# Two attention blocks: folded weight products moved ahead of everything, loads in chunks, biases as rows

## The chip, the cores and the metric

The kernel runs on one core of a Trainium2 chip. The metric is device time in microseconds (us), as the median of runs of the whole program. All data are 32-bit floats. The engines are TensorE (PE in the profile, with its weight loads shown apart as PEld), VectorE (DVE), ScalarE (ACT), GpSimd (POOL) and SyncE (SP), which here only issues transfers. Matmuls write to PSUM, of which this kernel uses banks under two tags, "s" and "o", with two buffers each; a buffer holds two banks of 128x512.

## The reference

Two blocks run one after the other on x of shape (8, 512, 32, 32): eight images, 512 channels, 1024 positions.

```python
# block 0: group norm of 32 groups, 8 heads of 64
h = group_norm(x, norm_w, norm_b)
qkv = einsum('oc,bchw->bohw', qkv_w, h) + qkv_b
attn = softmax(einsum('bhnd,bhmd->bhnm', q, k) / sqrt(64))
o = einsum('bhnm,bhmd->bhnd', attn, v)
x = x + einsum('oc,bchw->bohw', proj_w, o) + proj_b
# block 1: norm over the whole sample, one head of 512
n = norm(x) * gn_gamma + gn_beta
q, k, v = wq @ n + bq, wk @ n + bk, wv @ n + bv
attn = softmax(einsum('bci,bcj->bij', q, k) * 512**-0.5)
out = einsum('bcj,bij->bci', v, attn)
x = x + wo @ out + bo
```

## The kernel before

**Folded weights.** Block 1 has one head, so its query and key weights are multiplied into one matrix, "wqk1", and its value and output weights into another, "wvo1". `product` (L513) makes each of them on the chip by 16 matmuls of 128x512, which the trace shows as 32 passes, since a matmul of 32-bit floats is two. The biases that result are also made on the chip. `bias_through` (L485) multiplies a 512x512 matrix by a bias vector: 16 matmuls of a 128x128 stationary tile with a moving operand of one column (32 passes). It is used for "bias1" (wo1 with the value bias), "bias_q1" (nk1 with the query bias) and "bias0" (block 0's projection with its value bias).

**Strassen-like multiplication.** All large weight multiplications go through `strassen` (L369), with seven products instead of eight. A weight is held as a `Weight` tile of seven parts. A11, A12 and A22 are loaded, A21 goes to a tile called "rest", and `finish` (L171) makes S1 to S4 from them with four DVE operations. `Weight.finish` (L205) also writes the tile to DRAM ("stored"), and later images load it from there. There are three buffers for weight tiles. On the side of the data, `Combined` makes T1 to T4 from the quarters of x. `strassen` takes a bank tagged "s" (the line) and one tagged "o" (the single), copies the line out on ACT and adds on DVE.

**Order.** PE, ACT and DVE follow the order of the program text (a manual schedule). `at_steps` runs the steps of one or two interleaved multiplications and calls hooks between them, so work of other stages is put between the steps by hand. Before the first image:

1. SP loads nv1 and wo1, ACT's queue loads x of image 0; then the weights qk02 (ACT) and v0 (SP), then nq1 (ACT) and nk1 (SP). At most eight transfers are in flight: each issue waits for the one eight places earlier.
2. DVE takes the statistics of x (`of_half`, L291).
3. PE makes wvo1 and bias1, then the mean and variance products (L262); DVE and GpSimd turn them into scale and shift, and ACT and DVE normalise x (`normed`, L330, L332).
4. DVE finishes qk02 and v0 and makes T1 to T4; PE runs the first q and k stage (`pairs_qk`, heads' pairs 0 and 2).

Image 0 then runs `layer0`. First comes the value stage (`make_v`), between whose steps DVE takes the statistics of the next image's x. Only for image 0, `product` then makes wqk1 and bias_q1, the weights qk13 and p0 are finished, and bias0 is made. The second q and k stage (pairs 1 and 3) follows, then the attention: scores (L606), exponentials (L533), sums (L535), values (L625) and key sums (L639). The latter multiply by a tile of ones with 32 columns, which land in four different strips of 32 partitions. The projection (ps_p, L432) and block 1 come last. Images 1 to 7 repeat this with stored weights.

SP's transfers keep their own order; each waits for what it stores, for the buffer it fills, and for the transfer eight places earlier.

Of the kernel before, what the change touches and what calls it, by code (L numbers as in the profile page):

```python
# [40 lines left out]
P = 128  # L41
# [18 lines left out]
def two_attention_blocks(  # L60
# [3 lines left out]
    x: bass.AP,  # L64
    w_qkv0: bass.AP,
    w_proj0: bass.AP,
    n_q1: bass.AP,
# [22 lines left out]
    def banks(tag, name):  # L90
        return psum.tile([P, 2, HALF], FP, tag=tag, name=name)

    def tile2(name):
        return tpool.tile([P, 2, HALF], FP, tag="t", name=name)
# [18 lines left out]
    def load_x(b, queue):  # L113
        xs = quarters_of(f"x_{b}")
        for half in range(2):
            for i in range(2):
                queue.dma_start(xs[i][half], quarter_of(x, b, i, half))
        return xs

    def load_raw(src, name, queue):  # L120

        chunks = []
        for half in range(2):
            t = tile2(f"{name}_{half}")
            rows = src[half * 2 * P : (half + 1) * 2 * P]
            queue.dma_start(t, rows.rearrange("(cc p) o -> p cc o", p=P))
            chunks += [t[:, 0, :], t[:, 1, :]]
        return chunks

    vec = const.tile([P, 12 * NC], FP, tag="vec", name="vec")  # L130
    nc.scalar.dma_start(vec, vectors)
    nv1, wo1 = load_raw(n_v1, "nv1", nc.sync), load_raw(w_o1, "wo1", nc.sync)
    xs_next = load_x(0, nc.scalar)

# [45 lines left out]
    class Weight:  # L180

        def __init__(self, name, sources):
            self.name, self.sources = name, sources
            self.tile = wpool.tile([P, W_SIZE], FP, tag="w", name=f"w_{name}")
            self.parts, self.rest, at = [], [], 0
            for src, col, width in sources:
                size = len(A_PARTS) * 2 * width
                self.parts.append(parts_of(self.tile[:, at : at + size], width))  # L190
                at += size
            if name in stored:
                nc.sync.dma_start(self.tile, stored[name])

        def load(self, queue):
            for (src, col, width), parts in zip(self.sources, self.parts):
                rest = tile2(f"rest_{self.name}")[:, :, :width]
                self.rest.append(rest)
                for i in range(2):
                    for j in range(2):  # L200
                        cols = src[j * 2 * P : (j + 1) * 2 * P, i * 2 * P + col : i * 2 * P + col + width]
                        to = rest if (i, j) == (1, 0) else parts[f"A{i + 1}{j + 1}"]
                        queue.dma_start(to, cols.rearrange("(k p) o -> p k o", p=P))

# [5 lines left out]

    WQ0, WK0, WV0 = (w_qkv0[:, i * C : (i + 1) * C] for i in range(3))
    SOURCES = {
        "qk02": [(WQ0, 0, P), (WK0, 0, P)],
        "qk13": [(WQ0, P, P), (WK0, P, P)],
        "v0": [(WV0, 0, 2 * P)],
        "p0": [(w_proj0, 0, 2 * P)],
        "wqk1": [(None, 0, 2 * P)],
        "wvo1": [(None, 0, 2 * P)],
    }

    def load_first(name, queue):
        w = Weight(name, SOURCES[name])
        w.load(queue)
        return w

    waiting = [load_first("qk02", nc.scalar), load_first("v0", nc.sync)]
    nq1, nk1 = load_raw(n_q1, "nq1", nc.scalar), load_raw(n_k1, "nk1", nc.sync)


# [6 lines left out]
    def next_weight():  # L236

        w = waiting.pop(0)
        if coming:
            name = coming.pop(0)  # L240
            waiting.append(Weight(name, SOURCES[name]) if name in stored else load_first(name, nc.sync))
        return w
# [241 lines left out]

    def bias_through(w, v_bias, bias, name):  # L485


        t = const.tile([P, NC], FP, tag=name, name=name)
        ps = banks("s", f"ps_{name}")[:, 0, :]
        for oc in range(NC):  # L490
            for cc in range(NC):
                nc.tensor.matmul(  # L492
                    ps[:, oc : oc + 1], w(cc, oc), vec[:, v_bias + cc : v_bias + cc + 1],
                    start=cc == 0, stop=cc == NC - 1,
                )
        if bias is None:
            nc.vector.tensor_copy(t, ps[:, :NC])
        else:
            nc.vector.tensor_tensor(t, ps[:, :NC], vec[:, bias : bias + NC], ALU.add)
        return t  # L500

    def square_of(chunks):
        return lambda cc, oc: chunks[cc][:, oc * P : (oc + 1) * P]

    def square_of_parts(w):
        def square(cc, oc):
            i, j = oc // 2, cc // 2
            a = w.rest[0] if (i, j) == (1, 0) else w.parts[0][f"A{i + 1}{j + 1}"]
            return a[:, cc % 2, oc % 2 * P : (oc % 2 + 1) * P]

        return square

    def product(a, b, name):  # L513

        w = Weight(name, SOURCES[name])
        w.rest = [tile2(f"rest_{name}")[:, :, : 2 * P]]
        for j in range(2):
            ps = banks("o", f"ps_{name}_{j}")
            for k in range(2):
                to = 2 * j + k  # L520
                for cc in range(NC):
                    nc.tensor.matmul(  # L522
                        ps[:, k, :], a[cc][:, to * P : (to + 1) * P], b[cc],
                        start=cc == 0, stop=cc == NC - 1,
                    )
            evacuate(w.parts[0][f"A1{j + 1}"], ps[:, :, : 2 * P])
            evacuate(w.parts[0]["A22"] if j else w.rest[0], ps[:, :, 2 * P :])
        w.finish()

# [48 lines left out]
    def layer0(bs, qs, ks, b, load_next, norm_next):  # L578
# [12 lines left out]
        if b == 0:  # L591
            product(nq1, nk1, "wqk1")
            made["bias_q1"] = bias_through(square_of(nk1), V_BQ1, None, "bias_q1")

# [59 lines left out]
        if b == 0:  # L654
            w.finish()
            waiting[0].finish()
            made["bias0"] = bias_through(square_of_parts(waiting[0]), V_BV0, V_BP0, "bias0")
        hooks = {8: [lambda: score(0)], 9: [lambda: score(1)]}
# [25 lines left out]
        for i in range(2, len(units) + 2):  # L684
# [25 lines left out]
            if pair in spreads and (g, kt) == (1, NT - 1):  # L710
                for g in range(2):
                    divide(pair, g, spreads[pair][:, g, :])

        bias = made["bias0"]

# [193 lines left out]

    made = {}  # L910


    with tc.manual_schedule(engines={PE, ACT, DVE}):
        norm = norm0(xs_next, 0)
        for cc in range(NC):
            norm.of_half(cc, 0)
            norm.of_half(cc, 1)
            norm.of_channels(cc)
        product(nv1, wo1, "wvo1")
        made["bias1"] = bias_through(square_of(wo1), V_BV1, V_BO1, "bias1")  # L920
        norm.mean_of_all()
        norm.variance_of_all()
        norm.normed(xs_next)
        for w in waiting:
            w.finish()
        bs = combined(xs_next, "0_0")
        qs, ks = [None] * NC, [None] * NC
        at_steps(together(*pairs_qk(next_weight(), 0, bs, qs, ks, 0)), {})
        for b in range(B):
# [443 lines left out]
```

## Time and profile before

| | |
|---|---|
| runs | 2965.56, 2965.85, 2968.4 us; median 2965.85 |
| profiled execution: time | 2973.16 us |
| profiled execution: span | 2971.3 us |
| mean granted clock of TensorE | 0.993 |
| first matmul of the program | 10.33 us after the span's start |
| first value stage of image 0 | from 67.23 us |
| wqk1's product | from 91.40 us |
| second q and k stage of image 0 | from 116.31 us |

Durations are read from the profiled execution, and places in it are us from its span's start. A wait is idle time of an engine just before an instruction, with the engine and line, or the transfer, that ended it. PE's passes overlap, so the duration of one is longer than the time from one to the next; costs of PE are taken from start to start. The granted clock is a column of its own in the tables of windows.

### The profile page before, as it was taken

Reading aid. Unit: us, or ns where it says so; the run is one execution under the profiler, and the core shown is the slowest. Engines: PE = TensorE matmul, PEld = TensorE weight load, DVE = VectorE, ACT = ScalarE, POOL = GpSimd, SP = SyncE. Lnnn points to the kernel's source line nnn. Section 1 sums busy time; section 2 is a strip of 40 time slices with the busy share of each in tenths; the row PEclk is TensorE's granted clock in tenths of the full one; section 3 lists DMA queues with packets and bytes.
Section 4 is the critical chain, followed back from the end, with each engine's and each line's share of the span. In section 5 each row is a group of like instructions: output and inputs, shape, how many; then the busy total and the mean of one; then the engine's idle time right before and its main releaser. Section 6 shows DMA issues by size and latency. Waiting matters only on the chain.

```text
span 2971.3 us, 34006 instructions
## 1 busy us (share of the span) xinstructions
PE 2931.3 (99%) x14082; PEld 1375.2 (46%) x14082; DVE 1754.8 (59%) x2138; ACT 1067.6 (36%) x1505; POOL 13.9 (0%) x26
## 2 busy tenths in 40 slices
PE   7999999999999999999999999999999999999898
PEld 4633545335453455434553345533545335453353
DVE  3477355773657726586366843678445783547835
ACT  1264222632236321462215622165222642226421
POOL 0000000000000000000000000000000000000000
PEclk9999999999999999999999999999999999999999
DMA  7311213002130112201122020310212112121001
GB/s 244 112 56 33 75 43 128 15 33 75 54 116 19 54 50 91 80 22 50 50 92 86 15 74 25 117 61 15 75 50 92 64 30 82 43 79 36 8 0 37
DMA packets 61714, 184.22 MB, mean 62 GB/s; under 512 B 7024, under 2 KB 13168, under 8 KB 55152
## 3 DMA queue, kind: packets, MB, share of 16 engines
q1 hardware_dynamic: 57600, 177.76, 17.6%
q10 hardware_dynamic: 3952, 4.22, 0.4%
q8 instruction: 112, 1.84, 0.3%
q14 instruction: 50, 0.41, 0.0%
HBM read 137.39 MB, written 27.79 MB: 56 GB/s over the span
## 4 chain that ended last, share of the span: by engine, by line
PE 93%; DVE 5%; DMA 1%; SPq 0%; issue 0%; ACT 0%; POOL 0%; DVEq 0%; POOLq 0%; ACTq 0%
PE s L606 14%; PE ps_o L625 13%; PE ps_q L432 13%; PE ps_v L447 13%; PE ps_o L862 13%; PE ps_s L805 13%; PE ps_k L432 7%; PE ps_p L432 4%; DVE inv L546 2%; DVE acc L535 1%; PE ps_sum L639 1%; PE ps_wvo L522 1%; SPq L555 0%; PE ps_wqk L522 0%; PE ps_bias L492 0%
## 5 line engine op out<-in xcount | busy, mean ns | idle before, releaser
L533 ACT ACTIVATE p<-s 128x1024 f32<-128x1024 f32 x512 | 523.8, 1025 | 314.5 <-PE s L606 311.8
L606 PE MATMUL s<-q,k 64*64 64x512 f32 x4096 | 532.6, 591 | 0.0
L625 PE MATMUL ps_o<-p,v 64*64 64x512 f32 x4096 | 528.7, 589 | 0.0
L535 DVE TENSOR_TENSOR acc<-acc,p 128x1024 f32<-128x1024 f32 x384 | 468.4, 1220 | 79.8 <-ACT p L533 63.0
L606 PEld LDWEIGHTS s<-q,k 64*64 64x64 f32 x4096 | 151.9, 133 | 295.1 <-issue 254.0
L625 PEld LDWEIGHTS ps_o<-p,v 64*64 64x64 f32 x4096 | 156.6, 133 | 282.8 <-issue 280.3
L813 DVE TENSOR_TENSOR p<-ps_s,u_s 128x512 f32<-128x512 f32 x96 | 66.4, 692 | 249.1 <-ACT u_s L379 139.4
L481 DVE TENSOR_TENSOR v<-ps_v,u_v 128x512 f32<-128x512 f32 x96 | 66.2, 690 | 200.3 <-PE ps_v L447 130.5
L379 ACT COPY u_q<-ps_q 128x512 f32<-128x512 f32 x96 | 56.3, 586 | 334.4 <-PE ps_q L432 334.4
L379 ACT COPY u_v<-ps_v 128x512 f32<-128x512 f32 x96 | 56.3, 586 | 326.3 <-PE ps_v L447 326.3
L805 PE MATMUL ps_s<-s_q,t 128*128 128x512 f32 x384 | 167.4, 592 | 0.0
L862 PE MATMUL ps_o<-t_p,s_v 128*128 128x512 f32 x384 | 166.1, 592 | 0.0
L535 DVE TENSOR_TENSOR acc<-p,p 128x1024 f32<-128x1024 f32 x64 | 78.4, 1225 | 98.9 <-ACT p L533 98.9
L432 PE MATMUL ps_p<-t_p,w_p 128*128 128x512 f32 x256 | 113.3, 595 | 6.6 <-DVE inv L546 6.6
L464 DVE SCALAR_TENSOR_TENSOR q<-ps_q,bias_q,u_q 128x512 f32<-128x512 f32 x48 | 36.0, 750 | 136.8 <-ACT u_q L379 74.8
L805 PEld LDWEIGHTS ps_s<-s_q,t 128*128 128x128 f32 x384 | 73.0, 190 | 91.8 <-issue 91.8
L862 PEld LDWEIGHTS ps_o<-t_p,s_v 128*128 128x128 f32 x384 | 73.0, 190 | 91.8 <-issue 89.9
L862 PE MATMUL ps_o<-p,v 128*128 128x512 f32 x256 | 113.3, 595 | 0.0
L447 PE MATMUL ps_v<-w_wvo,t 128*128 128x256 f32 x512 | 113.1, 379 | 0.0
L432 PE MATMUL ps_q<-t,w_wqk 128*128 128x512 f32 x256 | 112.5, 592 | 0.0
L805 PE MATMUL ps_s<-q,h 128*128 128x512 f32 x256 | 112.5, 592 | 0.0
L546 DVE RECIPROCAL inv<-ps_sum 128x512 f32<-128x512 f32 x32 | 107.4, 3356 | 7.2 <-ACT held_sum L542 7.2
(200 smaller groups left out, 3627.7 us busy)
## 6 DMA issues: line engine op xcount, KB each, us to landing
x<-in_x SPq DMA_DIRECT2D x88, 512.0 KB, 7.4
w_qk<-stored_qk SPq DMA_DIRECT2D x14, 1792.0 KB, 7.3
out<-x SPq DMA_DIRECT2D x32, 512.0 KB, 2.8
w_wqk<-stored_wqk SPq DMA_DIRECT2D x8, 1792.0 KB, 7.5
w_wvo<-stored_wvo SPq DMA_DIRECT2D x8, 1792.0 KB, 7.6
w_v<-stored_v SPq DMA_DIRECT2D x7, 1792.0 KB, 7.5
w_p<-stored_p SPq DMA_DIRECT2D x7, 1792.0 KB, 7.1
inv<-inv SPq DMA_DIRECT2D x192, 64.0 KB, 2.0
```

The lines of the kernel that those rows point to most:

```text
L379: nc.scalar.copy(us[n], line)
L432: nc.tensor.matmul(bank, w[a][:, k, c * P : (c + 1) * P], bs[b][:, k, :], start=fresh and k == 0, stop=k == 1, skip_group_check=True,)
L447: nc.tensor.matmul(bank[:, u * 2 * P : (u + 1) * 2 * P], bs[b][:, k, n * P : (n + 1) * P], w[a][:, k, :], start=fresh and u == k == 0, sto ...
L481: nc.vector.tensor_tensor(v, pairs(bank), pairs(u), ALU.add)
L533: nc.scalar.activation(p, s, AF.Exp, scale=factor)
L535: nc.vector.tensor_tensor(acc, first, p, ALU.add)
L546: nc.vector.reciprocal(inv, ps)
L606: nc.tensor.matmul(s[cols, j, :], flat(ks[pair])[rows, k0 : k0 + HD], qs[pair][rows, g, :], start=True, stop=True,)
L625: nc.tensor.matmul(o[cols, half, :], vs[kt][rows, c0 : c0 + HD], p[rows, j, :], start=kt == 0, stop=kt == NT - 1,)
L805: nc.tensor.matmul(bank, bs[b][:, k, t * P : (t + 1) * P], q_parts[a][:, k, :], start=fresh and k == 0, stop=k == 1, skip_group_check=True,)
L813: nc.vector.tensor_tensor(p, bank, u, ALU.add)
L862: nc.tensor.matmul(bank, v_parts[kt // 2][a][:, kt % 2, c * P : (c + 1) * P], p_parts[kt // 2][b][:, kt % 2, :], start=fresh and kt == 0, ...
```

## The change

The change concerns what is done before image 0's attention.

- All first loads go on SP's queue, in order of use: nv1 and wo1 in chunks of 128 rows in turn, two chunks each of nq1 and nk1, x, the other chunks, then qk02. The weights of block 0 come in a layout prepared on the host, so that each part needs one transfer of long rows and one for "rest".
- `product` loops over the chunks of the sum outside and over the four output blocks inside, so that it can begin with the first chunk. Both products stand ahead of the first q and k stage: wvo1 in the "o" banks, wqk1 in the "s" banks. The mean and variance products of x come between wqk1's last matmuls. ACT alone evacuates both.
- Biases: `Through` copies each bias chunk to 32 columns on DVE, multiplies with it as the stationary operand of 128x32 and the weight as the moving one, and so gets four partial rows in four strips of 32 partitions. ACT copies them out, SP stores the four rows to DRAM and fetches each back as columns (elements of four bytes), and DVE adds the four shares.
- qk02 is finished between T2 and T3 of x; wqk1 and v0 are finished in hooks of the first q and k stage. v0 is loaded after wvo1 is stored.
- For image 0, after the value stage, the sums of bias1 and bias_q1 come on DVE, then qk13 and p0 are finished, then bias0's rows are multiplied. bias0's shares are added ahead of the projection.

```diff
+    for cc in range(NC):
+        load_raw(nv1, n_v1, cc)
+        load_raw(wo1, w_o1, cc)
+    for cc in range(2):
+        load_raw(nq1, n_q1, cc)
+        load_raw(nk1, n_k1, cc)
+    xs_next = load_x(0, nc.sync)
+    for cc in range(2, NC):
+        load_raw(nq1, n_q1, cc)
+        load_raw(nk1, n_k1, cc)
...
+        def load(self):
+            to = at = 0
+            for width in self.widths:
+                size = 2 * width
+                nc.sync.dma_start(self.tile[:, to : to + 3 * size], self.src[:, at : at + 3 * size])
+                rest = flat(tile2(f"rest_{self.name}"))[:, :size]
+                nc.sync.dma_start(rest, self.src[:, at + 3 * size : at + 4 * size])
...
-    def bias_through(w, v_bias, bias, name):
...
-        for oc in range(NC):
+    class Through:
+        def __init__(self, moving, v_bias, bias, name, ps):
+            self.bias, self.name, self.ps = bias, name, ps
+            many = tile2(f"many_{name}")[:, 0, :P].rearrange("p (c m) -> p c m", c=NC)
+            at = vec[:, v_bias : v_bias + NC]
+            nc.vector.tensor_copy(many, at.unsqueeze(2).to_broadcast([P, NC, P // NC]))
             for cc in range(NC):
+                for to, w in moving(cc):
+                    rows = ps[cc * (P // NC) : (cc + 1) * (P // NC), to]
+                    nc.tensor.matmul(rows, many[:, cc, :], w, start=True, stop=True)
+        def store(self):
+            row = tile2(f"row_{self.name}")[:, 0, :]
+            nc.scalar.copy(row, self.ps)
+            self.shares = dram.tile([NC, C], FP, tag=self.name, name=f"shares_{self.name}")
+            for cc in range(NC):
+                nc.sync.dma_start(self.shares[cc : cc + 1], row[cc * (P // NC) : cc * (P // NC) + 1, :])
+        def fetch(self):
+            self.columns = const.tile([P, NC, NC], FP, tag=f"c_{self.name}", name=f"c_{self.name}")
+            for cc in range(NC):
+                nc.sync.dma_start(
+                    self.columns[:, cc, :], self.shares[cc].rearrange("(o p) -> p o", p=P)
+                )
+        def add(self):
+            t, c = const.tile([P, NC], FP, tag=self.name, name=self.name), self.columns
+            nc.vector.tensor_tensor(c[:, :2, :], c[:, :2, :], c[:, 2:, :], ALU.add)
+            nc.vector.tensor_tensor(t, c[:, 0, :], c[:, 1, :], ALU.add)
+            if self.bias is not None:
+                nc.vector.tensor_tensor(t, t, vec[:, self.bias : self.bias + NC], ALU.add)
+            made[self.name] = t
+    def product(w, a, b, tag, between=()):
...
+        for cc in range(NC):
+            for to in range(NC):
                 nc.tensor.matmul(
+                    ps[to // 2][:, to % 2, :], a[cc][:, to * P : (to + 1) * P], b[cc],
                     start=cc == 0, stop=cc == NC - 1,
                 )
+                if cc == NC - 1 and to % 2 and between:
+                    between.pop(0)()
...
         if b == 0:
-            product(nq1, nk1, "wqk1")
-            made["bias_q1"] = bias_through(square_of(nk1), V_BQ1, None, "bias_q1")
+            for through in throughs:
+                through.add()
...
         if b == 0:
             w.finish()
             waiting[0].finish()
-            made["bias0"] = bias_through(square_of_parts(waiting[0]), V_BV0, V_BP0, "bias0")
...
+            throughs[:] = [Through(moving, V_BV0, V_BP0, "bias0", banks("s", "ps_bias0")[:, 0, :])]
+            throughs[0].store()
+            throughs[0].fetch()
...
-        product(nv1, wo1, "wvo1")
-        made["bias1"] = bias_through(square_of(wo1), V_BV1, V_BO1, "bias1")
-        norm.mean_of_all()
-        norm.variance_of_all()
+        wvo1 = Weight("wvo1")
+        product(wvo1, nv1, wo1, "o")()
+        waiting.append(load_first("qk02"))
+        wqk1 = Weight("wqk1")
+        wvo1.finish()
+        spare[0] = banks("o", "ps_norm")[:, 0, :]
+        taken = product(wqk1, nq1, nk1, "s", [norm.mean_of_all, norm.variance_of_all])
+        spare[0] = None
+        ps = banks("o", "ps_biases")
+        everywhere = slice(0, C)
+        throughs += [
+            Through(lambda cc: [(everywhere, wo1[cc])], V_BV1, V_BO1, "bias1", ps[:, 0, :]),
+            Through(lambda cc: [(everywhere, nk1[cc])], V_BQ1, None, "bias_q1", ps[:, 1, :]),
+        ]
         norm.normed(xs_next)
-        for w in waiting:
-            w.finish()
-        bs = combined(xs_next, "0_0")
+        taken()
+        waiting.append(load_first("v0"))
+        for through in throughs:
+            through.store()
+        combine = Combined("0_0")
+        combine.first(xs_next)
+        waiting[0].finish()
+        combine.second()
+        bs = combine.parts
         qs, ks = [None] * NC, [None] * NC
-        at_steps(together(*pairs_qk(next_weight(), 0, bs, qs, ks, 0)), {})
+        w = next_weight()
+        at_steps(
+            together(*pairs_qk(w, 0, bs, qs, ks, 0)), {2: [wqk1.finish], 8: [waiting[0].finish]}
+        )
+        for through in throughs:
+            through.fetch()
```

## The prediction

> **What bounds the kernel now.** I read the page first: the engines' shares, then the chain that ended last.
>
> ```profile
> span 2971.3 us, 34006 instructions
> PE 2931.3 (99%) x14082; PEld 1375.2 (46%) x14082; DVE 1754.8 (59%) x2138; ACT 1067.6 (36%) x1505; POOL 13.9 (0%) x26
> ...
> PE 93%; DVE 5%; DMA 1%; SPq 0%; issue 0%; ACT 0%; POOL 0%; DVEq 0%; POOLq 0%; ACTq 0%
> ```
>
> TensorE (PE) is busy throughout; so only time in which PE waits, does work that need not be done, or runs slowly can be won. All that the diff touches lies before 140 us. So the next view is what PE waited for in the first 150 us, and then windows of 2 us (length; busy time and count of PE, its weight loads, DVE, ACT, GpSimd; then the granted clock, 1.00 is full; DMA share; GB/s).
>
> ```profile
> PE ps_wvo L522 <- DMA wo<-in_w_o: 10.3, 1, 10.3
> PE ps_q L432 <- DVE q L464: 3.4, 1, 3.4
> PE ps_q L432 <- DVE x L332: 2.8, 1, 2.8
> PE ps_v L262 <- DVE spread L306: 0.9, 1, 0.9
> ```
>
> ```profile
> 34.00:36.00 2.00, 0.00 (x0) 0.00 (x0) 1.05 (x5) 0.56 (x1) 0.81 (x1) 0.50 1.05 444
> ...
> 110.00:112.00 2.00, 2.00 (x11) 2.00 (x11) 1.93 (x7) 0.00 (x0) 0.00 (x0) 0.50 1.09 459
> ...
> 118.00:120.00 2.00, 2.00 (x4) 0.81 (x3) 0.00 (x0) 0.00 (x0) 0.00 (x0) 0.50 0.86 230
> ```
>
> Four waits make 17.4 us. Beside them, the 128x1 bias products run the clock down: it is 0.50 at 34 us and from about 108 to 121 us although PE counts as busy. The timeline shows the stretch after the first value stage:
>
> ```profile
> 91.40 13.90 PE L522 MATMUL ps_wqk<-nk,nq 128*128 128x512 f32 x32
> ...
> 105.14 4.48 PE L492 MATMUL ps_bias_q<-vec,nk 128*128 128x1 f32 x32
> ...
> 109.48 3.55 PE L492 MATMUL ps_bias<-vec,w_p 128*128 128x1 f32 x16
> ...
> 116.31 6.18 PE L432 MATMUL ps_q<-x,w_qk 128*128 128x512 f32 x8
> ```
>
> Product 13.7 us, two biases 11.2 us, then eight passes in 6.0 us (122.32 - 116.31) where eight at full clock take 8 x 0.43 = 3.4: 2.6 lost to the clock. From the end of the value stage (91.40) to work at full clock this stretch costs 24.9 + 2.6 = 27.5 us.
>
> **First stretch: start to the value stage (PE at 67.23 us before).** Before, the first product waits until 10.33 for whole matrices. After, its first four matmuls need one 256 KB chunk of each. Loads begin to move at about 2.5 us and run at 370 to 395 GB/s in the trace, so 512 KB are there by 2.5 + 1.4, plus landing: 4.5 us taken, 4.3 to 5.5. The product takes 16.4 as before (10.33 to 26.74, its slow first six passes of 0.86 included): 20.9. It is not starved: all 2 MB land by about 8.5. The second product follows at once, 13.7: 34.6; its last chunks, behind x on the same queue, are 6.3 MB into the stream, 2.5 + 17 = 19.5 us, needed at 27.8. The statistics of x (8 x 0.69 on DVE, done near 20) and the evacuation and sums of the first product (ACT 4 x 0.59, DVE 4 x 0.69, done near 25) hide beside it. Without that cover they would cost 2.4 + 2.8. The mean goes in after 28 of 32 passes, the variance after all: its chain of small DVE operations (1.1 us, by the row pair 130.91 to 131.97) hides under four passes of 1.7. That ends the 0.9 wait.
>
> The new order makes new waits. Variance product at 34.8; by the same chain of the next image (132.85 to 135.22) scale and shift are there 2.4 later, 37.2. PE is next to do the bias rows, which wait for the spread-out vectors, two DVE copies queued behind the shift: nearest rows 128x4 at 0.16 and 128x256 at 0.42; 0.3 taken. PE idle 2.7. The rows: eight passes each with 32 columns at four different strips; the nearest row is the key sums of the attention:
>
> ```profile
> 178.31 1.06 PE L639 MATMUL ps_sum<-acc,ones 128*32 128x512 f32 x8
> ```
>
> Eight such passes start the next work 1.0 us later (179.31), so bias1 and bias_q take 2.0, to 39.5. If strips did not overlap it were 16 x 0.43 = 6.9; I take 2.0, the same shape. Then the first q line needs the bank of the second product's first half. ACT empties it only behind its four normalisations: 37.2 + 2.9 (row L330, x4 in 2.93) + 2 x 0.59 = 41.3. So PE idles 1.8 more, and the old 2.8 wait is replaced by 4.5. The normalised x, T1 and T2 and the eight qk02 sums (2.9) are done on DVE by about 45.5, and T4 by 48; PE wants the first sum at 41.3 + 6.9 = 48.2: the 3.4 wait is gone, with under 3 us to spare, beyond which it returns one for one. The stage is 24.0 long (chain, ps_q L432 x56): 65.3.
>
> The clock: an idle 3.42 us at 44.84 was followed by 0.50 in the window 50 to 52, and resumptions at 36.04 and 116.31 cost 1.7 and 2.6 us. Waits of 2.7 and 1.8 around 2.0 of work are nearest to these: 2.0 taken, 0 to 3.4. The value stage starts at 67.3: no gain, 0.1 lost.
>
> (The Trainium skill, TensorE: Matmul & The Clock Gate, Part 1, has the half clock come back after at least one idle window of about 3.4 us. By that rule neither wait alone lowers the clock, this term would be 0 and the forecast 2947.7; the trace's 0.50 after 3.42 us of idling does not decide it for shorter waits.)
>
> **Second stretch.** No product and no bias_q behind the value stage. But bias0's rows wait for their vector, and DVE has this in front of it, by the rows of 91.60 and 109.74 to 115.27: last value 0.8 after the stage's end, five small bias sums 1.0, qk13's sums 2.9, p0's sums 2.6, copy 0.3: 7.6 us in which PE idles. Before, PE's own product covered these sums. Then bias0: 16 passes of 256 columns, four strips, at half clock 1.7; the clock needs 3.3 to 5.0 us from resumption (36.04 to 39.3, 116.31 to 121.3), so 1.3 more is lost in the next stage. 10.6 against 27.5: 16.9 gained. p0 and the next x load behind the column fetches on SP's queue; p0 has 18 us to spare.
>
> **The rest.** bias0's three small sums (3 x 0.2) stand on DVE before the first output projection, which waits for DVE's reciprocal: 0.6 lost. Beyond, order and operations are the same on every engine. Queues: SP now issues all loads, 0.3 to 0.5 us each, less than the 0.7 us that 256 KB take at 370 GB/s. It then waits at the bias rows' stores, and 12 column fetches of four-byte elements follow; stored wqk, qk13 and the next x stand behind the first eight. Loads of 512-byte rows moved 188 GB/s, about 370 packets per us: 512 elements 1.4 us, so eight cost 11, from about 47 to 58. x then lands near 72, wanted on DVE at 74.5, with 7 us more before it holds PE.
>
> (The Trainium skill, DMA: Bandwidth & Descriptors, Bandwidth, asks for transfers of at least 1 MiB. An estimate from its fit under Anatomy of one DMA, 2.0 us plus bytes/436e3, is 2.6 us for each chunk; eight in file would land by 22 and end the first product near 25 instead of 20.9, total 2954. The trace, with many smaller loads in flight at 370 GB/s, speaks against it.)
>
> Sum: +0.1 - 16.9 + 0.6 = -16.2. The profiled execution: span 2971.3 becomes 2955.1, its own time 2973.16 becomes 2957.0. That execution lies 7.3 above the median 2965.85; carried to the median: 2949.7.
>
> **The rivals.** (1) Strips do not overlap: the first rows end at 44.4, 3.1 later than the bank is free, and bias0 takes 3.4 to 6.9 instead of 1.7: 6.5 lost, 2956. Against it: the row at 178.31. (2) No change: the moved product costs in the first stretch what it saves in the second. That takes a q stage starting 10 us later, at 51, so loads of some 150 GB/s on the one queue, 2960 to 2968. Against it: SP alone moved x at 394 GB/s from 58 to 60. (3) Slower: the four-byte fetches hold SP. Stalls begin when eight end after 73 (3.3 us each, in file), and each us beyond costs PE one; the gain is gone at 5.3 each and it is slower by over 0.2% from 6.0; at 8 each it ends at 111, 38 past the point, 2987. The nearest small transfers land in 2.0 (inv) and 2.9 us (vec), with eight in flight. No row of four-byte elements exists, so this is the unknown. That the change is not what it says can be left out: the order of instructions shows both products before the first q.
>
> **How the numbers follow.** Forecast 0.73, with 2945 to 2955 its own range (start, clock terms). Rival 1 0.12, a milder delay of the first stretch that stays under 2960 0.05, rival 2 0.05, rival 3 0.05. A measurement can tell about 0.2% (5.9 us) from no change: faster 0.90, same 0.05, slower 0.05. Range 2943 to 2960: down by no clock loss and the strips' bounds, up to rival 1's far end of 8.3 plus a late start.
>
> **What would show it.** Right: PE starts near 4.5; waits of about 2.7, 1.8 and 7.6 on DVE, ACT, DVE; value stage near 67; second q stage near 101; granted clock 0.50 after the long wait. Wrong: bias rows of 3 us, a DVE wait on the next x, or the value stage after 72.

## The result, and the profile after

| | before | changed |
|---|---|---|
| median of four runs each, us | 2967.06 (2965.56 to 2968.4) | 2952.64 (2952.05 to 2953.6) |
| profiled execution: time, span, us | 2973.16, 2971.3 | 2953.6, 2951.9 |

The ratio is 0.9952, with a 95% interval from 0.9935 to 0.9969: faster by 14.4 us. The forecast was 2949.7, with a range from 2943 to 2960. The kernel before varies more than the changed one: over its 34 runs in this study it took 2965.56 to 2973.32, with medians of 2969.89 to 2971.57 in the later comparisons, where the changed kernel stayed at 2953. So a gain of 18 us in a later comparison is no larger effect of the change.

First the page of the changed kernel: the span, the engines' shares and the chain that ended last.

```profile
span 2951.9 us, 33920 instructions
PE 2916.8 (99%) x14018; PEld 1359.2 (46%) x14018; DVE 1752.8 (59%) x2142; ACT 1069.7 (36%) x1512; POOL 13.9 (0%) x26
...
PE 94%; DVE 4%; ACT 1%; issue 0%; SPq 0%; DMA 0%; POOL 0%; DVEq 0%; POOLq 0%
```

The span is 19.4 us shorter and PE's busy time 14.5. There are 64 passes fewer, since three biases of 32 passes have become three of 8 or 16. PE is still what bounds the kernel. Next, PE's waits in the first 150 us.

```profile
PE ps_bias L504 <- issue: 7.2, 1, 7.2
PE ps_wvo L536 <- DMA wo<-in_w_o: 4.7, 1, 4.7
PE ps_biases L504 <- DVE many_bias_q L500: 2.4, 1, 2.4
PE ps_q L438 <- ACT rest_wqk L546: 0.2, 1, 0.2
```

The four old waits made 17.4 us, these make 14.5. Three of the old ones are gone and the wait for the first load is less than half. The waits that replace them, for spread-out vectors and for a bank, make 9.8. The longest is put down to "issue", but the timeline shows what it is. Its columns are start, duration, engine, line and instruction, and in brackets the idle time before it.

```profile
4.68 16.83 PE L536 MATMUL ps_wvo<-wo,nv 128*128 128x512 f32 x32 [4.68 <-DMA wo<-in_w_o]
...
38.03 1.94 PE L504 MATMUL ps_biases<-wo,many_bias 128*32 128x512 f32 x8 [2.44 <-DVE many_bias_q L500]
39.70 1.78 PE L504 MATMUL ps_biases<-nk,many_bias_q 128*32 128x512 f32 x8
41.71 3.70 PE L438 MATMUL ps_q<-x,w_qk 128*128 128x512 f32 x8 [0.23 <-ACT rest_wqk L546]
65.85 7.07 PE L453 MATMUL ps_v<-w_v,x 128*128 128x256 f32 x32
97.03 0.22 DVE L500 COPY many_bias<-vec 128x128 f32<-128x128 f32 x1
97.36 1.11 PE L504 MATMUL ps_bias<-w_p,many_bias 128*32 128x256 f32 x8 [7.17 <-issue]
99.24 5.35 PE L438 MATMUL ps_q<-x,w_qk 128*128 128x512 f32 x8
104.43 3.60 PE L438 MATMUL ps_k<-x,w_qk 128*128 128x512 f32 x8
```

The bias rows of 97.36 start right behind DVE's copy of 0.22 at 97.03, which stands last of all in DVE's work there. The rows of 38.03 and 39.70 take 1.7 each from start to start. The second q stage begins at 99.24 (before 116.31), and its first eight passes need 5.2 us (104.43 - 99.24), where eight at full clock take 3.4. The windows show why (the clock is the column of its own ahead of the last two):

```profile
38.00:40.00 2.00, 1.97 (x12) 0.68 (x16) 1.84 (x5) 2.00 (x4) 0.00 (x0) 0.50 0.00 0
42.00:44.00 2.00, 2.00 (x6) 0.80 (x6) 1.97 (x6) 1.86 (x5) 0.00 (x0) 1.00 0.04 9
...
94.00:96.00 2.00, 0.00 (x0) 0.00 (x0) 1.97 (x5) 0.00 (x0) 0.00 (x0) 0.50 1.00 430
...
98.00:100.00 2.00, 2.00 (x15) 0.76 (x7) 0.00 (x0) 0.59 (x1) 0.00 (x0) 0.50 1.02 437
```

The clock is 0.50 while the bias rows run, and again from 92.4 to 102.6, that is through the long wait and into the second q stage. After 42 us and after 103 us it is 1.00. Of the slow stretch before, 108 to 121 us, nothing is left but this.

### The profile page after: what moved, and what is told of

It reads as the page before. It is cut to its first block, busy times and chain, and to the rows that moved or that the text cites. A ratio compares the mean times of both kernels' runs of the same rounds, so it can differ in the third digit from the quotient of the medians.

```text
span 2951.9 us, 33920 instructions
## 1 busy us (share of the span) xinstructions
PE 2916.8 (99%) x14018; PEld 1359.2 (46%) x14018; DVE 1752.8 (59%) x2142; ACT 1069.7 (36%) x1512; POOL 13.9 (0%) x26
## 4 chain that ended last, share of the span: by engine, by line
PE 94%; DVE 4%; ACT 1%; issue 0%; SPq 0%; DMA 0%; POOL 0%; DVEq 0%; POOLq 0%
PE s L626 15%; PE ps_o L645 14%; PE ps_q L438 13%; PE ps_v L453 13%; PE ps_o L893 13%; PE ps_s L836 13%; PE ps_k L438 7%; PE ps_p L438 4%; DVE inv L566 1%; DVE acc L555 1%; PE ps_sum L659 1%; PE ps_wvo L536 1%; PE ps_wqk L536 0%; DVE t_p L705 0%; DVE t_p L711 0%
```

## The experiments

**The theory.** The gain comes from the order: both products fill PE while the loads, the statistics and the sums run, so that three waits go, and the second stretch loses its product. The rows save little, since they bring waits of their own. The rivals: the rows carry the gain; or the loads in chunks do; and the waits that came in cost nothing, or cost what they show.

Beyond the result, the kernels were timed in three comparisons, each beside the kernel before: up to "order only" (its median 2971.57), up to "loads as before" (2971.14), and the last two (2969.89). The changed kernel stood only in the first. So a distance of a later kernel from it holds to about the 2 us between those medians, and the places in the traces, which do not have this doubt, are given beside it.

Places and spans of the profiled executions, and the medians of all runs, in us:

| kernel | value stage | second q stage | first scores | span | median |
|---|---|---|---|---|---|
| before | 67.23 | 116.31 | 140.03 | 2971.3 | 2967.06 |
| before, again | 65.36 | 114.54 | 138.16 | 2969.6 | 2971.57 |
| changed | 65.85 | 99.24 | 122.14 | 2951.9 | 2952.64 |
| changed, again | 65.23 | 98.62 | 121.25 | 2951.4 | 2953.14 |
| rows only | 63.80 | 103.76 | 126.43 | 2958.2 | 2960.07 |
| order only | 73.11 | 100.77 | 122.00 | 2951.6 | 2953.7 |
| without the second wait | 65.93 | 91.22 | 112.46 | 2942.3 | 2943.8 |
| without the first waits | 63.15 | 96.54 | 118.87 | 2951.3 | 2952.29 |
| without both | 62.77 | 88.06 | 109.30 | 2941.0 | 2943.04 |
| loads as before | 68.37 | 101.77 | 124.49 | 2954.7 | 2956.45 |
| fetches four times | 65.17 | 106.97 | 128.78 | 2958.2 | 2959.99 |
| bias0 twice | 72.86 | 106.07 | 130.32 | 2961.4 | 2962.06 |

**The kernel before and the changed one, again.** The kernel before was profiled a second time, and both were timed beside the variants.

> The kernel before once more, unchanged, for a second profile. The first profiled execution of it (2973.16 us) lies 6 us above the median of its runs, and the difference of the two profiled spans (19.4) is larger than that of the medians (14.4). If the first execution only met the clock at a bad moment, the new profile has the value stage's end to full clock of the second q stage at 27.5 us less up to 3, and the excess is in the first 140 us. If it is spread over the images, the first 140 us are the same and the later landmarks drift.

> The changed kernel, unchanged, timed beside the others of this call: 2952.6 us, 14 below the kernel before. The theory and its rivals say the same here; it is the mark for the others.

Measured: 2971.28 for the one execution of the kernel before, 2953.14 (2951.12 to 2954.41) for the changed one, against 2971.57 (2968.15 to 2973.32); the ratio is 0.9939 (0.9925 to 0.9952). The second execution of the kernel before has the same 72.8 us from the value stage to the first scores as the first one. It is ahead by 1.9 at the value stage and by 1.7 at the end, so the two differ almost wholly in what lies ahead of the value stage. There the first product takes 15.4 instead of 16.4, and bias1's 32 one-column passes 3.5 instead of 4.4 (the first execution's line, then the second's):

```profile
26.74 4.58 PE L492 MATMUL ps_bias<-vec,wo 128*128 128x1 f32 x32
```

```profile
25.78 3.63 PE L492 MATMUL ps_bias<-vec,wo 128*128 128x1 f32 x32
```

In the first one the clock fell to 0.50 under these passes, 2.4 us after they began; in the second it stayed at 1.00 to their end.

In the second execution of the changed kernel, too, the clock went another way at the same place. Timeline and windows:

```profile
37.41 1.06 PE L504 MATMUL ps_biases<-wo,many_bias 128*32 128x512 f32 x8 [2.45 <-DVE many_bias_q L500]
38.26 1.07 PE L504 MATMUL ps_biases<-nk,many_bias_q 128*32 128x512 f32 x8
41.09 3.70 PE L438 MATMUL ps_q<-x,w_qk 128*128 128x512 f32 x8 [1.76 <-ACT rest_wqk L546]
```

```profile
38.00:40.00 2.00, 1.33 (x15) 0.16 (x4) 1.81 (x4) 2.00 (x4) 0.00 (x0) 1.00 0.00 0
...
94.00:96.00 2.00, 0.00 (x0) 0.00 (x0) 1.97 (x4) 0.00 (x0) 0.00 (x0) 0.66 0.96 409
```

Here the rows start 0.85 apart at full clock, and PE then waits 1.76 for ACT. In the first execution they start 1.67 apart at half clock, and PE waits 0.23. From the first row to the first q both take 3.68: it is ACT that sets the time of the first q, and the half clock only eats into the wait. The same wait of 2.4 ahead of the rows stands in three of the variants below: the clock fell there in "without the second wait", and stayed at 1.00 in "loads as before" and "fetches four times". The value stages differ by 0.6, which is what their products differ by already.

**Rows only.** The order and the loads of the kernel before; each `bias_through` is replaced by rows in its old place, with vectors spread out ahead of everything.

```diff
-        made["bias1"] = bias_through(square_of(wo1), V_BV1, V_BO1, "bias1")
+        rows_of(lambda cc: [(everywhere, wo1[cc])], "bias1", V_BO1)
...
-            made["bias0"] = bias_through(square_of_parts(waiting[0]), V_BV0, V_BP0, "bias0")
+            rows_of(moving, "bias0", V_BP0)
```

> The old order and the old loads, with the biases as rows of 128x32 products, their spread-out vectors made at the start, so that no row waits for DVE. My theory (both parts gain much the same time, the 27.5 us behind the value stage, so they do not add): product 13.7, bias_q and bias0 about 2 instead of 11.2, full clock (2.6 won), then 1.8 of waiting for DVE's sums and 1.6 more for the bias sums ahead of the projection: 9 to 11 below the kernel before, 2956 to 2958. Rival, the biases are the whole gain: 2952.6. Rival, the order is the whole gain: 2967. In the profile the granted clock stays at 1.00 from the value stage on.

Measured: 2960.07 (2958.32 to 2962.92), ratio 0.9965 (0.9951 to 0.9978), 11.5 below the kernel before. The size of the drop is just above what was named; the level is higher because the kernel before ran slower in this comparison. The value stage comes 3.4 and 1.6 earlier than in the two executions of the kernel before. PE's waits in the first 150 us show why the first stretch does not gain all that bias1 saves:

```profile
PE ps_wvo L535 <- DMA wo<-in_w_o: 10.4, 1, 10.4
PE ps_q L432 <- DVE q L464: 4.5, 2, 3.4
PE ps_v L262 <- DVE spread L306: 3.5, 1, 3.5
PE ps_q L432 <- DVE x L332: 2.8, 1, 2.8
```

bias1 takes 1.0 instead of 4.4, and the wait behind it for the statistics grows from 0.9 to 3.5. The gain is in the second stretch: the value stage's start to the first scores is 62.6 instead of 72.8, because 64 one-column passes of 11.2 become rows of 2.0 and the next stage runs at full clock, less a new wait of 1.2 for DVE in that stage.

**Order only.** The changed kernel with the old one-column biases, in the places where the rows were.

```diff
-            Through(lambda cc: [(everywhere, wo1[cc])], V_BV1, V_BO1, "bias1", ps[:, 0, :]),
-            Through(lambda cc: [(everywhere, nk1[cc])], V_BQ1, None, "bias_q1", ps[:, 1, :]),
+            bias_through(square_of(wo1), V_BV1, V_BO1, "bias1", ps[:, 0, :]),
+            bias_through(square_of(nk1), V_BQ1, None, "bias_q1", ps[:, 1, :]),
...
-            throughs[:] = [Through(moving, V_BV0, V_BP0, "bias0", banks("s", "ps_bias0")[:, 0, :])]
+            bias_through(
+                square_of_parts(waiting[0]), V_BV0, V_BP0, "bias0", banks("s", "ps_bias0")[:, 0, :]
+            )()
```

> The new order and the new loads, with the biases as 128x1 products in the places of the rows (no DRAM, no spread-out vectors; DVE takes bias1 and bias_q1 out behind T4). My theory: 64 passes take about 12 us instead of the two waits and rows between the variance product and the first q (6.4), at a falling clock, so the value stage starts 7 to 8 us later than after's 65.9; behind the value stage 32 passes need no DVE and run while DVE makes its sums: the second q stage is 3 us nearer. Net 4 above after: 2957. Rival, the order is the whole gain: 2952.6. Rival, the biases are the whole gain: 2967.

Measured: 2953.7 (2951.69 to 2955.8), ratio 0.994 (0.9927 to 0.9954): the same as the changed kernel. The expectation of 4 us more was wrong. The timeline:

```profile
35.26 5.00 PE L497 MATMUL ps_biases<-vec,wo 128*128 128x1 f32 x32
40.12 6.96 PE L497 MATMUL ps_biases<-vec,nk 128*128 128x1 f32 x32
46.95 5.73 PE L438 MATMUL ps_q<-x,w_qk 128*128 128x512 f32 x8
...
97.28 1.84 PE L497 MATMUL ps_bias<-vec,w_p 128*128 128x1 f32 x16
...
100.77 3.68 PE L438 MATMUL ps_q<-x,w_qk 128*128 128x512 f32 x8
```

The first biases take 11.7 (35.26 to 46.95) and the value stage comes 7 to 8 later than in the changed kernel. The second stretch gives all of it back: 48.9 from the value stage to the first scores instead of 56.3 and 56.0. bias0's one-column passes need only vectors that have long been there and the raw parts of the weight, not its sums, so they follow the value stage without a wait. They take 3.5 at full clock, and the passes behind them 3.5: 7.0 from 97.28 to 104.29. The window in their middle:

```profile
98.00:100.00 2.00, 2.00 (x21) 2.00 (x20) 1.94 (x6) 0.00 (x0) 0.00 (x0) 1.00 0.84 222
```

The changed kernel needs 7.2 for the wait, 1.9 for rows and 5.2 for the same passes, 14.2. So the rows win 7 to 8 us in the first stretch and lose as much in the second. On the whole they bring nothing as they stand in the changed kernel, and the order and the loads make its gain. Rows in the first place with one-column passes in the second were not run.

**Without the second wait.** bias0's vector is spread out before the first matmul instead of behind the sums of p0.

```diff
+        for name, at in [("bias0", V_BV0)]:
+            manies[name] = spread_out(at, name)
...
-            throughs[:] = [Through(moving, V_BV0, V_BP0, "bias0", banks("s", "ps_bias0")[:, 0, :])]
+            throughs[:] = [Through(moving, manies["bias0"], V_BP0, "bias0", banks("s", "ps_bias0")[:, 0, :])]
```

> The changed kernel with bias0's spread-out vector made on DVE at the start instead of behind the sums of qk13 and p0; nothing else. My theory (the wait of 7.2 us and the half clock behind it are pure loss that the order of DVE makes): bias0 starts as the value stage ends, about 90, takes 0.9, the second q stage starts at about 91 at full clock instead of 99.2 and half: 9 to 10 less, 2943. DVE's sums (to 97) then lie beside the first four products of the stage, which end at about 97.8. Rival, the sums are needed at once and the wait only moves to the first product with S1: 2950 to 2952, with PE waiting some 6 us for DVE w_qk or q in that stage.

Measured: 2943.8 (2941.32 to 2944.36), ratio 0.9907 (0.9892 to 0.9922), 9.3 below the changed kernel's 2953.14.

```profile
90.20 0.66 PE L502 MATMUL ps_bias<-w_p,many_bias 128*32 128x256 f32 x8
...
91.22 3.70 PE L438 MATMUL ps_q<-x,w_qk 128*128 128x512 f32 x8
94.76 3.60 PE L438 MATMUL ps_k<-x,w_qk 128*128 128x512 f32 x8
```

No idle time stands before the rows. They take 1.0 instead of 1.9, and the eight passes 3.5 instead of 4.9 to 5.2. 7.2 of wait, 0.9 in the rows and 1.4 to 1.7 in the passes account for the 9.3 within half a us, and from the value stage to the first scores it is 46.5 instead of 56.3 and 56.0. The rival's wait for DVE does not show. One copy of 0.22 us at the end of DVE's queue had cost that much.

**Without the first waits.** The vectors of bias1 and bias_q are spread out early; ACT empties wqk1's banks ahead of its normalisations; T3 and T4 move behind the first steps of the q and k stage.

```diff
-        norm.normed(xs_next)
         taken()
+        norm.normed(xs_next)
...
-        combine.second()
...
+            together(*pairs_qk(w, 0, bs, qs, ks, 0)), {1: [combine.second], 2: [wqk1.finish], 8: [waiting[0].finish]}
```

> The changed kernel with three edits in the first stretch: the vectors of bias1 and bias_q1 spread out at the start, wqk1's banks emptied by ACT ahead of its normalisations, and T3 and T4 made behind the first q and k results on DVE. My theory (two waits, 2.4 and the bank until 41.7, replaced by the wait for the normalised x): rows at 35.5 to 37.2, q from about 38.5, S1 at 46.0 instead of 48.7 because DVE's sums and the first q bound it: 2.7 less, 2950. Rival, DVE's chain from the scale to the sums bounds the stage in any case: 0 to 0.7 less, 2952 to 2952.6.

> The edits of the two kernels before together. My theory: the two stretches follow each other on PE, so the gains add: 12 to 13 less than the changed kernel, 2940, some 27 below the kernel before. Rival: the second stretch is bound by loads of qk13 and p0 or the next x, which an earlier start does not move: less than the sum, 2943 to 2945.

Measured: 2952.29 (2951.41 to 2954.11) without the first waits alone, and 2943.04 (2942.07 to 2943.88) without both, ratio 0.9907 (0.9892 to 0.9922). That is 0.8 below the kernel that each is to be compared with (2953.14 and 2943.8), less than what the first stretch won. That stretch did what it was to do: the value stage starts 2.1 to 2.7 earlier, at 63.15, with waits of 1.1 and 0.6 in place of 2.4 and 1.8. The theories' 2950 and 2940 were missed all the same, and both rivals named about the right time for a wrong reason: DVE's chain did not hold the first stretch, and without both waits the second stretch is as long as without the second alone (46.5 from the value stage to the first scores). The lead of 2.1 to 3.1 us is still there ahead of the last projection of the last image. There PE's wait is longer (the line of the changed kernel's second execution, then that without the first waits):

```profile
2769.02 3.27 PE L438 MATMUL ps_p<-t_p,w_p 128*128 128x512 f32 x7 [0.50 <-DVE inv L566]
```

```profile
2767.24 4.99 PE L438 MATMUL ps_p<-t_p,w_p 128*128 128x512 f32 x11 [1.77 <-DVE inv L570]
```

1.3 go there, and 1.3 more in the statistics and the q stage behind it, where the granted clock was 0.87 over 40 us instead of 0.91; but the first execution of the changed kernel has 0.87 there, too. Without both waits the last wait is 1.70. In the seven other executions with the new order it is 0.50, also without the second wait, where the lead is larger; so an earlier start alone does not bring it on. Waits of this kind do scatter (1.36 at the seventh image of the changed kernel's second execution). Whether the edits lengthen the last one, and how, is open; no run was made for it. The kernel without both waits is the fastest found, some 28 below the kernel before, but not to be told apart from the one without the second alone.

**Loads as before.** All of nv1 and then all of wo1, still in transfers of 128 rows; x on ACT's queue, and the sum of the first product on the inside loop again. The order of the stages, the rows and the prepared layout of block 0's weights are the changed ones.

```diff
     for cc in range(NC):
         load_raw(nv1, n_v1, cc)
+    for cc in range(NC):
         load_raw(wo1, w_o1, cc)
...
-    xs_next = load_x(0, nc.sync)
+    xs_next = load_x(0, nc.scalar)
```

> The changed kernel with the first loads in the old manner: all of nv1 and then all of wo1 on SP, x at the same time on ACT's queue, and the first product with the sum inside, so that its first matmuls need chunks of both matrices whole. My theory (the start of the first product lies on the path one for one): the first matmul waits for 1.3 MB and a share of x, starts at 6.5 to 9 instead of 4.7, and the whole program is later by that difference, 2 to 4 us: 2955 to 2957. Rival, the early start only fills a wait for the statistics or for x: 2952.6, with the first q at 41.7 as before.

Measured: 2956.45 (2955.08 to 2957.23), ratio 0.9951 (0.9937 to 0.9964), 3.3 above the changed kernel, as expected. PE's waits in the first 150 us have this line on top, 2.9 more than in the changed kernel, and the value stage comes 2.5 and 3.1 later than in its two executions:

```profile
PE ps_wvo L539 <- DMA wo<-in_w_o: 7.5, 1, 7.5
```

So the loads in order of use bring about 3 of the gain, near one for one with the first wait. This kernel is 14.7 below the kernel before of its comparison; that is the order, with rows that bring nothing on the whole. No run has the order alone with the old loads, and none takes back the prepared layout of the weights.

**Fetches four times.** The eight column fetches of bias1 and bias_q are issued three more times, into tiles that nobody reads.

```diff
+            for n in range(3 if self.name != "bias0" else 0):
+                more = const.tile([P, NC, NC], FP, tag=f"c{n}_{self.name}", name=f"c{n}_{self.name}")
+                for cc in range(NC):
+                    nc.sync.dma_start(
+                        more[:, cc, :], self.shares[cc].rearrange("(o p) -> p o", p=P)
+                    )
```

> The changed kernel with the eight column fetches of bias1 and bias_q repeated three more times into tiles that nobody reads: 32 fetches instead of 8 on SyncE, ahead of the store of the product, the sums of the next stage's weights and the next x. It quadruples the one cost that the prediction's slower rival rests on. The eight took 6.9 us of SP's queue (47.4 to 54.4). My theory: the queue serves them in file, so 32 take about 28 us and end near 75; the next x is issued near 82 to 90 instead of 61.8 and lands 15 later, at 97 or after; DVE wanted it at 73.6 and has some 7 us of slack, so PE is held 10 to 17 us in the second q stage: 2963 to 2970. Rival theory: fetches to different tiles run beside each other and only their issue counts, 32 x 0.3 = 10 us, or the slack is larger than I think: 2951 to 2955, no new wait on the next x.

Measured: 2959.99 (2959.64 to 2960.6), ratio 0.9967 (0.9955 to 0.998): about 7 above the changed kernel, between the two theories. SP's queue of the changed kernel, then of this one:

```profile
47.44 4.16 SPq L516 DMA_DIRECT2D c_bias<-shares_bias  x4
51.65 2.64 SPq L516 DMA_DIRECT2D c_bias_q<-shares_bias_q  x4
...
61.80 2.21 SPq L119 DMA_DIRECT2D x<-in_x  x4
```

```profile
46.75 4.15 SPq L516 DMA_DIRECT2D c_bias<-shares_bias  x4
50.94 2.66 SPq L522 DMA_DIRECT2D c_bias<-shares_bias  x4
...
77.74 2.36 SPq L119 DMA_DIRECT2D x<-in_x  x4
```

The queue does serve them one behind the other, the first eight at 0.7 to 1.0 each, and the next x is issued 15.9 later (16.6, counted from the start of the value stage). The 32 took 26 us of the queue, 0.5 to 1.1 each. The wait came at another place than expected, in the value stage and not in the second q stage (PE's waits):

```profile
PE ps_v L453 <- DVE v L487: 6.1, 1, 6.1
```

On DVE the statistics of the next x stand ahead of sums of the value stage. DVE waits 12.2 for x, does not take the values out of their banks, and PE stands:

```profile
85.26 0.69 DVE L297 BATCH_NORM_STATS2 part<-x 128x6 f32<-128x512 f32 x1 [12.23 <-DMA x<-in_x]
```

16.6 later minus 6.1 of wait leaves 10.5 us of slack in the changed kernel. The half clock behind that wait costs the value stage 2.1 more.

**bias0 twice.** The variant "order only", with bias0's 32 one-column passes issued twice.

```diff
-        for oc in range(NC):
+        for oc in list(range(NC)) * (2 if name == "bias0" else 1):
```

> The variant with the new order and loads and one-column bias products (2953.7), with bias0's 32 products behind the value stage issued twice: 64 instead of 32, the second set overwriting the first with the same numbers. In the variant the 32 took 3.49 us at full clock and cost nothing in the stage behind; in the kernel before, 64 such products at the same place ran at 0.50 from about 2.7 us after their start until 5 us after their end. My theory: one-column products count as idle time for the clock although PE shows busy, and a stretch of them longer than about 3 to 3.5 us lowers it, waits or not. Then 64 take 11 us and the next eight passes lose 2 to 2.6 more: 9 to 11 above the variant, 2962 to 2965. Rival theory: only waits of PE (the ones that the kernel before had) lower the clock: 32 more products cost 3.5 at full clock, 2957, and the granted clock stays at 1.00.

Measured: 2962.06 (2958.44 to 2964.17), ratio 0.9971 (0.9959 to 0.9982), 8.4 above "order only" (8.6 by the places from the value stage to the first scores): the theory's mechanism, at a little less than its 9 to 11. Windows:

```profile
98.00:100.00 2.00, 2.00 (x20) 2.00 (x20) 1.93 (x6) 0.00 (x0) 0.00 (x0) 1.00 0.92 222
...
102.00:104.00 2.00, 2.00 (x12) 2.00 (x11) 1.39 (x3) 0.00 (x0) 0.00 (x0) 0.50 1.02 417
...
110.00:112.00 2.00, 2.00 (x3) 0.67 (x2) 0.00 (x0) 0.45 (x1) 0.00 (x0) 0.50 0.94 401
```

PE shows as busy throughout and waits for nothing here; the clock falls to 0.50 about 4.9 us after the first one-column pass (97.03), and is back near 112. The passes of the stage behind lose 3.1 (6.55 instead of 3.44). So the rival, that only waits lower the clock, is out.

## Why the prediction was right, and where it was off

**Where the time went.** In the two profiled executions the value stage starts 1.4 earlier, value stage to first scores is 16.5 shorter (72.8 to 56.3), and 1.5 more comes behind: 19.4. The prediction had 0.1 later, 16.9 shorter and 0.6 longer: 16.2. The main term, the second stretch, was right in its parts: wait 7.6 forecast and 7.2 measured, rows 1.7 and 1.9, clock lost behind them 1.3 and 1.5 to 1.75.

**First stretch.** The places of PE, forecast and measured: first matmul 4.5, 4.68; end of wvo1 20.9, 21.35; end of wqk1 34.6, 35.3; wait for the vectors 2.7, 2.73 when counted, as there, from the start of the variance product (2.44 of it idle); first q 41.3, 41.71 and 41.09; first sum product 48.2, 48.68; no old wait came back. The step that failed is the clock term of 2.0 added to the value stage: 67.3 was forecast, 65.85 and 65.23 measured. The half clock did come, in one execution of the two. But it fell on the rows, and these stood in front of a wait for ACT, which took it up: 3.45 of rows and 0.23 of wait in one, 1.92 and 1.76 in the other, 3.68 in both. The prediction, too, had the first q wait for ACT (until 41.3), but it put the clock on top of that.

The Trainium skill (TensorE: Matmul & The Clock Gate, Part 1) would have made this term 0, which was the better number, but for a reason that the runs do not bear out. It asks for an idle window of about 3.4 us, and the clock fell here after some 2.2 us of idle time (at 37.8). The same section says that the window runs freely and does not begin with the kernel. The delay does vary: at the wait for bias0 the clock fell 2.2 us after PE had stopped in one execution and 5.1 in the other. But the 2.2 is again less than one such window.

**Loads.** The chunks moved as counted; the first product ended at 21.35. The estimate in the prediction from the fit of the Trainium skill (DMA: Bandwidth & Descriptors, Anatomy of one DMA) would have put it near 25, with eight chunks one behind the other. The page has the fit for transfers issued from GpSimd, while these are issued from SP, and up to eight are in flight; for them the measurement decides against it. The run with the old loads prices the order of the loads at about 3; transfers of 1 MiB were not tried.

**The rest.** 0.6 was to be lost at the first projection, to bias0's sums. Its wait is 0.87 in both profiles of the changed kernel and was 1.92 and 1.70 before, so nothing was lost there. The eight waits of that kind made 6.6 and 6.3 before, 4.7 and 5.5 after, and 4.2 to 6.2 in the variants; what sets each was not tried.

**From the execution to the median.** Here the prediction carried 7.3 over: the profiled execution of the kernel before lay that much above the median. The changed kernel's lies 1.0 above its own. Forecast for the profiled execution was 2957.0, measured 2953.6; for the median 2949.7, measured 2952.64. So the sum was 3.4 too high, and the carrying took off 6.3 too much. The two errors partly cancel, so that the median came within 2.9 us is in part luck. That the kernel before scatters over 8 us, and the changed one over 3.3, was not foreseen. 1.9 us of it show in the two executions, in the first product and under bias1's one-column passes; what else scatters is open.

**The rivals.** (1) Strips that do not overlap: ruled out by rows 0.85 apart for eight passes, where 3.4 would be needed. (2) A late start by the one queue: the run "loads as before" shows the opposite. (3) The four-byte fetches: eight took 6.9, where 11 were forecast. By the slack above, the stall begins with 10.5 us more on SP's queue: eight ending near 65 instead of 54, 2.2 each, and not at 73 or 3.3 each, as the prediction had it. Its own count for the next x (landed at 72, needed at 81.5) has a slack of 9.5, which was near and, behind fetches that end at 58, would have given 67.5; its price for the rival did not use it. At 0.9 each the fetches were still far from deciding.

## What to carry to other kernels

Look at what stands last in the queue of the engine that a new wait depends on: a copy of 0.22 us that needed only a vector loaded at the start cost 9.3 us, because it was issued behind 7 us of sums, and moving it brought more than half as much as the whole change. A cheaper form of an operation is worth only what its waits leave over: behind the value stage rows of 1.9 us replaced one-column passes of 3.5 us and lost 7 us, as the one-column form needed no help from DVE at that place; without the wait they win. A stretch at half clock costs nothing when a long enough wait for another engine stands behind it, so clock terms belong on the chain of waits, not on top of it.

## What the runs showed of the hardware

The granted clock falls under one-column passes as it does in waits, although PE shows as busy. Under 64 of them it fell to 0.50 in all five places where so many ran in one stretch (both executions of the kernel before, "order only", and twice in "bias0 twice"), 2.1 to 4.9 us after they began. Under 32 of them, 3.5 us at full clock, it fell in one place (bias1 in the first execution of the kernel before, after 2.4 us) and not in two (bias1 in its second execution, bias0 in "order only"). So the length alone does not decide it, and 32 are not safe.

Waits of 2.4 us lowered the clock in two of five executions with the wait ahead of the rows, and the wait of 7.2 us in all five that have it, 2.2 to 5.3 us after PE had stopped. Eight fetches of 512 four-byte elements, one behind the other on SP's queue, took 0.7 to 1.0 us of it each, bias0's four 0.5 each.
